# Four graph layers in one kernel: when a chunk of rows is finished, and how far ahead weight tiles are made

## The chip, the cores and the metric

The kernel runs on one core of a Trainium2 chip. The core's engines work side by side, each through its own queue of instructions: TensorE multiplies matrices (PE in the profile, PEld for its weight loads), VectorE (DVE), ScalarE (ACT) and GpSimd (POOL) do elementwise work, and SyncE (SP) issues DMAs; ACT and POOL issue some too. An engine that needs another's result waits for a semaphore. On-chip tiles lie in SBUF, and matmuls write to PSUM. The metric is the device time of one execution in microseconds.

## The reference

`x` has 2708 rows of 512 features, and `adj` is a symmetric 0/1 matrix of 2708 x 2708 with ones on its diagonal. Four layers follow one another, each of the form x = x + layer(relu(layernorm(x)), adj):

```python
# layer 0
support = a.T @ X;  out = relu((support @ weight) * deg**-0.5)
# layer 1: of each row the first 64 neighbours only
keep = Ab & (jnp.cumsum(Ab.astype(jnp.int32), axis=1) <= neibor_num)
nb_mean = (keep @ X) / jnp.maximum(cnt, 1.0)
out = leaky_relu(X @ W_line.T + b_line) + leaky_relu(nb_mean @ W_nb.T + b_nb)
# layer 2: attention with 8 heads of 64
attention = softmax(where(adj > 0, leaky_relu(f1[:, None] + f2[None, :]), -9e15))
out = elu(attention @ Wh)
# layer 3: mean over the neighbours, two linear maps, their concatenation through a third
agg = mask @ x / jnp.maximum(deg, 1.0)
out = relu(concatenate([x @ W_self + b_self, agg @ W_nb + b_nb]) @ W_comb + b_comb)
```

Layers 1 and 3 each multiply a masked adjacency matrix by a 2708 x 512 matrix. The change concerns these two multiplications.

## The kernel before

Rows are worked on in 22 chunks of 128; the last has 20 rows. Layer 0 also packs the adjacency pattern, and the pattern later lies on the chip as bytes (`vT`). Each of layers 1 and 3 has two stages. A dense stage goes through the chunks: it loads x, normalizes it, transposes it on TensorE and multiplies it by the weights. What is to be aggregated is split into two parts of fp32r (`halves`, L291), so that each product of the aggregation is two matmuls. In layer 1 this stage runs from the end of layer 0 to about 508 us.

The second stage is `aggregate` (L432). The chunks that are computed are grouped in seven spans of 4, 4, 4, 4, 3, 2 and 1 chunks (`cuts`, L108). For each span it makes 22 steps, one for each chunk `m` that is summed over. A step needs a weight tile `kt`, which holds the masked pattern between chunk `m` and the chunks of the span: 512, 384, 256 or 128 columns wide. In layer 1, `weight1` (L868) makes it on DVE by comparing `lastr` (the position up to which a row's neighbours are kept) with the index of the row, times the pattern. In layer 3, `weight3` (L1526) makes it by a cast of the pattern. Both pools hold three `kt` buffers. `multiply` then issues two matmuls for each chunk of the span (one where `m` is the short chunk) into that chunk's PSUM accumulator; these are line L424. Thus a step of a four-chunk span is eight matmuls, and one of the one-chunk span is two.

The lines of the program are written out in steps by `staged` (L250): at each step first `make` for the step that lies `lead` ahead, and then `multiply` for the own step. `lead` is 2 in both layers. `multiply` also does three other things. At step 11 it loads the rows of x that the span's result is added to (`before`). In the last span it starts the first three steps of layer 2's dense stage, at steps 9, 13 and 18 (`AHEAD`, L476). And in the first steps of a span it finishes the chunks of the span before, one in each step (`after`).

In layer 1 finishing a chunk (`after1`, L880) is: on DVE, scale the accumulator and add the bias (L883), then the leaky relu (L886), both into `y`; on POOL, add `y` to x (L890); and on the ACT queue, a DMA that saves x. The last span's own chunk is added on DVE. In layer 3 (`after3`, L1568) it is two DVE instructions (L1571, L1574) and the DMA to the output.

A planner orders the instructions of each engine's queue. It goes by the order in which the lines are written and by when it thinks that operands and buffers are there, so a `kt` can stand between L883 and L886 of a chunk, and work of layer 2 between the last steps of layer 1. Tiles of x lie in a ring of five buffers (`XBUFS`, L111), accumulators in a ring of eight PSUM banks. The tiles of layer 2, among them `parts` and `parts2` (L964 and L968, cleared by POOL), take over SBUF that layer 1's tiles held, and wait for the last use of those.

Of the kernel before, what the change touches and what calls it, by code (L numbers as in the profile page):

```python
# [9 lines left out]
F32R = mybir.dt.float32r  # L10
# [12 lines left out]
R = 128  # L23
# [21 lines left out]
def fast_layers(  # L45
# [63 lines left out]
    spans = [list(range(a, b)) for a, b in zip(cuts, cuts[1:])]  # L109
# [3 lines left out]
    WG = KMAX * R  # L113
# [136 lines left out]
    def staged(count, *stages, done=0):  # L250

        for step in range(done, count + max(lag for lag, _ in stages)):
            emit_step(step, count, stages)
# [157 lines left out]
    def pattern(m, cs, n=R):  # L411

        g, k = where[m]
        v = vT[g][:n, k, cs[0] * R : (cs[-1] + 1) * R]
        return v.rearrange("p (c r) -> p c r", r=R)

    def by_chunk(t, cs):
        return t[:, : len(cs) * R].rearrange("p (c r) -> p c r", r=R)

    def matmuls(acc, parts, weight, k, m):  # L420

        q = 2 if m < NC - 1 else 1
        for i in range(q):
            nc.tensor.matmul(  # L424
                acc[:R],
                weight[:, k * R : (k + 1) * R],
                parts[:, i, :],
                start=(m == 0 and i == 0),
                stop=(m == NC - 1),
            )  # L430

    def aggregate(weight_of, parts, before, after, lead=2, ahead=()):  # L432

        units = [(g, m) for g in range(len(spans)) for m in range(NC)]
        weight, loaded, acc = {}, {}, {}

        def make(i):  # L440
            g, m = units[i]
            weight[i] = weight_of(m, spans[g])

        def multiply(i):
            g, m = units[i]
            cs = spans[g]
            if m == 0:
                for c in cs:
                    acc[c] = ps.tile([P, D], F32, name="acc", tag="ps")
            for k, c in enumerate(cs):  # L450
                matmuls(acc[c], parts[m], weight[i], k, m)
            del weight[i]
            if m == NC // 2:
                loaded.update((c, before(c)) for c in cs)
            if g == len(spans) - 1:
                for at_m, fn, *args in ahead:
                    if m == at_m:
                        fn(*args)
            if g and m < len(spans[g - 1]):
                c = spans[g - 1][m]  # L460
                after(c, acc.pop(c), loaded.pop(c))

        staged(len(units), (0, make), (lead, multiply))
        for c in spans[-1]:
            after(c, acc.pop(c), loaded.pop(c))
# [7 lines left out]
    with ExitStack() as ring_ctx:  # L473
# [31 lines left out]
        with tc.tile_pool(name="l0", bufs=2) as wk, ExitStack() as ctx_l0:  # L505
            units = [(g, m) for g in range(len(groups)) for m in range(NC)]
            tiles, acc, sums, xs = {}, {}, {}, {}
# [254 lines left out]
        wk = ring_ctx.enter_context(tc.tile_pool(name="l1", bufs=1, side="right"))  # L762
# [3 lines left out]
        h1, turned = {}, {}  # L766
# [99 lines left out]
            nc.sync.dma_start(w2s[:, f], w2[:, f * P : (f + 1) * P, :].rearrange("h p o -> p h o"))  # L866

        def weight1(m, cs):  # L868
            kt = wk.tile([R, WG], F32R, name="kt", bufs=3)
            nc.vector.scalar_tensor_tensor(  # L870
                by_chunk(kt, cs),
                lastr[:, cs[0] * R : (cs[-1] + 1) * R].rearrange("p (c r) -> p c r", r=R),
                index[:R, m : m + 1],
                pattern(m, cs),
                op0=ALU.is_ge,
                op1=ALU.mult,
            )
            return kt
# [32 lines left out]
            scalar=True,  # L911
        )
        ahead = [(m, emit_step, step, NC, stages2) for step, m in enumerate(AHEAD)]
        aggregate(weight1, h1, before1, after1, ahead=ahead)

# [55 lines left out]
    row, weight, wh, whs, acc, sides, made, scaled = {}, {}, {}, {}, {}, {}, [], {}  # L973
# [499 lines left out]
    with ExitStack() as stack:  # L1473
# [34 lines left out]
        for c in range(NC):  # L1508
# [13 lines left out]
        wk = stack.enter_context(  # L1522
            tc.tile_pool(name="l3", bufs=2, side="right", reuse_waits="tile")
        )
# [645 lines left out]
def kernel(tc: tile.TileContext, *args: bass.AP):  # L2170

    nc = tc.nc
    with tc.tile_pool(name="verdict", bufs=1) as pool:
        verdict = pool.tile([1, 1], I32, name="verdict")
        fast_layers(tc, *args, verdict)
        odd = nc.values_load(verdict[0:1, 0:1], min_val=0, max_val=P + 1)
        with tc.If(odd > 0):
            general_layers(tc, *args)
# [32 lines left out]
```

## Time and profile before

| what | us |
|---|---|
| median of 3 runs (lowest, highest) | 1751.03 (1750.17, 1754.02) |
| the profiled execution | 1754.19 |
| its span, from the first instruction to the last | 1752.3 |
| PE busy | 1724.1 |
| DVE busy | 1312.2 |
| ACT busy | 845.6 |
| POOL busy | 248.3 |
| layer 1's aggregation, in the span's time | 507.9 to 728.9 |
| layer 3's aggregation | 1529.1 to 1745.2 |

In the page, a group of instructions has one row: line, engine and operation, output tile and input tiles, shapes, count, busy time and mean, and at its end the idle time of the engine just before these instructions and what ended it. The chain of work that ended last is followed back from the last instruction. The table by stretch cuts the span where one asks and gives each engine's busy time there, with the number of instructions in brackets. The timeline gives start, length, engine and line of each instruction or run of equal ones, and in square brackets the idle time before it.

### The profile page before, as it was taken

The numbers are of one execution on the slowest core, as the hardware profiler recorded it, in microseconds if no ns is written. First come the engines' busy times: TensorE is split into PE (matmuls) and PEld (weight loads), VectorE is DVE, ScalarE is ACT, GpSimd is POOL, SyncE is SP. The second block draws the span as 40 slices with busy tenths as digits, with TensorE's granted clock in tenths as the row PEclk, the third lists the DMA queues.
The fourth block names the chain that finished last, engine by engine and source line by source line (L and its number), as shares of the span: only waits on it lengthen the run. The fifth ranks groups of instructions, "written<-read, shape, count | busy, mean of one in ns | idle before, by whom it ended". The sixth has DMA issues, their size and how long they took to land.

```text
span 1752.3 us, 29486 instructions
## 1 busy us (share of the span) xinstructions
PE 1724.1 (98%) x11280; PEld 1078.8 (62%) x11280; DVE 1312.2 (75%) x1902; ACT 845.6 (48%) x1554; POOL 248.3 (14%) x252
## 2 busy tenths in 40 slices
PE   8999999999999999999999999999999999999998
PEld 5567777744468887644675665434434455588886
DVE  7759889855455556888899999999998677633334
ACT  5447777622210000366878888888794566400000
POOL 1003323311111112255000000000001222100000
PEclk9999999999999999999999999999999999999999
DMA  8436666444551111332420221022022444313221
GB/s 291 139 117 199 205 206 186 133 120 123 121 135 49 48 49 56 122 122 93 133 63 13 61 64 58 15 64 62 13 74 72 130 141 130 109 36 109 73 72 41
DMA packets 167227, 177.37 MB, mean 101 GB/s; under 512 B 84127, under 2 KB 106591, under 8 KB 166060
## 3 DMA queue, kind: packets, MB, share of 16 engines
q1 hardware_dynamic: 144428, 131.99, 27.2%
q10 hardware_dynamic: 18808, 33.37, 5.1%
q0 software_dynamic: 3840, 10.03, 1.5%
q8 instruction: 90, 1.47, 0.4%
q14 instruction: 61, 0.50, 0.1%
HBM read 111.64 MB, written 55.36 MB: 95 GB/s over the span
## 4 chain that ended last, share of the span: by engine, by line
PE 86%; DVE 8%; ACT 2%; issue 2%; DMA 1%; SPq 1%; POOL 0%; ACTq 0%; DVEq 0%; POOLq 0%
PE acc L424 36%; PE av L1297 17%; PE nb_ps L187 8%; DVE t L1067 5%; PE sums L1297 4%; PE h_ps L187 4%; PE line_ps L187 4%; PE self_ps L187 4%; PE hT_ps L245 2%; PE fused_ps L370 2%; PE wh_ps L187 1%; DVE wh_a L1114 1%; PE av_ps L1250 1%; ACT b L1085 1%; DVE f L1131 1%
## 5 line engine op out<-in xcount | busy, mean ns | idle before, releaser
L1067 DVE SCALAR_TENSOR_TENSOR t<-rb,ec,vT 128x2708 f32<-128x2708 f32 (+2 forms) x214 | 510.4, 2450 | 8.3 <-PE sums L1297 6.2
L1297 PE MATMUL av<-t,whs 128*32 128x451 f32 (+5 forms) x4432 | 445.5, 514 | 6.2 <-DVE t L1067 3.9
L424 PE MATMUL acc<-halves,kt 128*128 128x512 f32 x1848 | 426.5, 391 | 2.4 <-DVE kt L870 2.1
L424 PEld LDWEIGHTS acc<-halves,kt 128*128 128x128 f32 x1848 | 345.2, 188 | 79.7 <-DVE kt L870 6.6
L1085 ACT ACTIVATE b<-t,eb 128x2708 bf16<-128x2708 f32 (+1 forms) x119 | 285.0, 2395 | 33.3 <-DVE t L1067 33.2
L1297 PEld LDWEIGHTS av<-t,whs 128*32 128x32 f32 (+1 forms) x4432 | 193.2, 110 | 167.9 <-issue 118.5
L424 PE MATMUL acc<-halves,ar 128*128 128x512 f32 x924 | 243.6, 414 | 0.0
L424 PEld LDWEIGHTS acc<-halves,ar 128*128 128x128 f32 x924 | 172.6, 188 | 58.2 <-issue 20.6
L223 ACT ACTIVATE ln_rs<-ln_mv,eps 128x1 f32<-128x1 f32 x88 | 25.7, 295 | 306.3 <-DVE ln_mv L221 298.4
L870 DVE SCALAR_TENSOR_TENSOR kt<-lastr,index,vT 128x512 fp32r<-128x512 int16 (+3 forms) x154 | 112.5, 742 | 75.8 <-PE acc L424 75.4
L1528 DVE CAST kt<-vT 128x512 fp32r<-128x512 uint8 (+3 forms) x154 | 56.5, 368 | 131.3 <-PE acc L424 131.2
L1264 POOL TENSOR_SCALAR z<-y 128x512 f32<-128x512 f32 x22 | 44.1, 2005 | 639.5 <-DMA aT<-avT 513.6
L555 DVE TENSOR_TENSOR_SCAN cum<-ai,deg 128x512 int16<-128x512 int32 (+2 forms) x110 | 128.3, 1170 | 0.0
L598 ACT ACTIVATE cum<-cum,limit 128x512 int16<-128x512 int16 (+3 forms) x132 | 88.0, 667 | 51.6 <-DVE deg L563 49.4
L1297 PE MATMUL sums<-t,whs 128*32 128x325 f32 (+4 forms) x952 | 104.4, 451 | 0.0
L1051 ACT ACTIVATE whs<-wh,ef 128x64 f32<-128x64 f32 x214 | 72.5, 342 | 59.6 <-PE sums L1297 21.1
L219 DVE BATCH_NORM_STATS2 ln_st<-x 128x6 f32<-128x512 f32 x88 | 60.3, 687 | 48.3 <-DMA x<-x 34.1
L187 PE MATMUL nb_ps<-wfn,hT 128*128 128x512 f32 x168 | 78.7, 612 | 2.1 <-ACT hT L247 2.1
L187 PE MATMUL wh_ps<-w2s,hT 128*128 128x512 f32 x168 | 76.1, 595 | 1.0 <-ACT hT L247 0.9
L187 PE MATMUL h_ps<-w0s,hT 128*128 128x512 f32 x168 | 76.5, 598 | 0.0
L1297 PE MATMUL sums<-b,parts 128*32 128x338 bf16 (+2 forms) x884 | 76.0, 308 | 0.0
L549 ACT ACTIVATE ar<-ai 128x512 fp32r<-128x512 int32 (+2 forms) x132 | 75.0, 568 | 1.7 <-DMA ai<-in_adj 1.3
(211 smaller groups left out, 1952.7 us busy)
## 6 DMA issues: line engine op xcount, KB each, us to landing
x<-x SPq DMA_DIRECT2D x105, 256.0 KB
ai<-in_adj SPq DMA_DIRECT2D x84, 256.0 KB
x<-x ACTq DMA_DIRECT2D x84, 256.0 KB
x<-in_x SPq DMA_DIRECT2D x42, 256.0 KB
rb<-rT SPq DMA_DIRECT2D x7, 1354.0 KB
wh<-whd SPq DMA_DIRECT2D x63, 96.0 KB
packed<-two POOLq DMA_DIRECT2D x44, 128.0 KB, 3.3
whd<-wh SPq DMA_DIRECT2D x21, 256.0 KB
```

What stands on the lines that cost most here:

```text
L187: nc.tensor.matmul(po[:n], lhsT[:, f, :n], w[:, f, :], start=(f == 0), stop=(f == NF - 1))
L219: nc.vector.bn_stats(st[:n], xc[:n])
L424: nc.tensor.matmul(acc[:R], weight[:, k * R : (k + 1) * R], parts[:, i, :], start=(m == 0 and i == 0), stop=(m == NC - 1),)
L549: nc.scalar.activation(ar[:, :gw], ai[:, :gw], AF.Square, accum_out=squares[:R, m, g : g + 1])
L555: nc.vector.tensor_tensor_scan(cum[:n, :gw], ai[:n, :gw], ai[:n, :gw], 0.0 if g == 0 else deg[:n, m : m + 1], op0=ALU.add, op1=ALU.max,)
L598: nc.scalar.activation(cum[:n, :gw], cum[:n, :gw], AF.Sign, bias=limit[:n], scale=-1.0, accum_out=signs[:n, m, g : g + 1],)
L870: nc.vector.scalar_tensor_tensor(by_chunk(kt, cs), lastr[:, cs[0] * R : (cs[-1] + 1) * R].rearrange("p (c r) -> p c r", r=R), index[:R, m ...
L1051: ins = nc.scalar.activation(t[:q, :O], wh.pop((u, m))[:q], AF.Copy, scale=by)
L1067: ins = nc.vector.scalar_tensor_tensor(t[:q, : hi - lo], row[h][:q, lo:hi], ec[:q, m, h : h + 1], vT[g][:q, k, lo:hi], op0=ALU.max, op1=AL ...
L1085: nc.scalar.activation(b[:q, : hi - lo], weight[s][:, : hi - lo], AF.Sigmoid, bias=eb[:q, m, h : h + 1], scale=STEEP,)
L1297: nc.tensor.matmul(p[j * S : (j + 1) * S, : b - a], lhsT, rhs[:, part * size + a : part * size + b], start=(s % NC == 0), stop=(s % NC == ...
L1528: nc.vector.tensor_copy(by_chunk(kt, cs), pattern(m, cs))
```

## The change

Two edits are made. In `aggregate` a chunk of the span before is finished in each step while the new span has three or four chunks, as it was; in each second step where the span has two chunks (steps 0, 2 and 4 of layer 1's and layer 3's sixth span); and in each third step where it has one (steps 0 and 3 of the seventh). In layer 1 alone, weight tiles are made four steps ahead and their pool has five buffers. Layer 3 keeps two steps and three buffers.

```diff
@@ aggregate
-            if g and m < len(spans[g - 1]):
-                c = spans[g - 1][m]
-                after(c, acc.pop(c), loaded.pop(c))
+            if g:
+                k, off = divmod(m, 1 + 2 // len(cs))
+                if off == 0 and k < len(spans[g - 1]):
+                    c = spans[g - 1][k]
+                    after(c, acc.pop(c), loaded.pop(c))
@@ weight1
-            kt = wk.tile([R, WG], F32R, name="kt", bufs=3)
+            kt = wk.tile([R, WG], F32R, name="kt", bufs=5)
@@ the call in layer 1
-        aggregate(weight1, h1, before1, after1, ahead=ahead)
+        aggregate(weight1, h1, before1, after1, lead=4, ahead=ahead)
```

## The prediction

> **What bounds the kernel now.** I read the page's busy shares first, then its chain, then the table by stretch for the spans concerned, then the timeline inside them. From the page:
>
> ```profile
> span 1752.3 us, 29486 instructions
> PE 1724.1 (98%) x11280; PEld 1078.8 (62%) x11280; DVE 1312.2 (75%) x1902; ACT 845.6 (48%) x1554; POOL 248.3 (14%) x252
> L424 PE MATMUL acc<-halves,kt 128*128 128x512 f32 x1848 | 426.5, 391 | 2.4 <-DVE kt L870 2.1
> L424 PEld LDWEIGHTS acc<-halves,kt 128*128 128x128 f32 x1848 | 345.2, 188 | 79.7 <-DVE kt L870 6.6
> ```
>
> TensorE sets the time nearly everywhere. A matmul's end is modelled, so the 2.1 us on the first L424 row understates the waits on `kt`; the 6.6 us on the row of weight loads overstates them, since part of each is hidden under matmuls still in flight. The table by stretch, for instructions that touch `kt` (length, PE busy, weight loads, DVE busy), settles it; the rows are layer 1's wide spans, its two-chunk and one-chunk spans, then layer 3's two-chunk and one-chunk spans:
>
> ```profile
> 507.90:693.30 185.40, 185.40 (x817) 152.90 (x817) 88.50 (x109) 1.00 0.19 58
> 693.30:714.80 21.50, 20.17 (x87) 15.79 (x86) 11.93 (x23) 1.00 0.24 76
> 714.80:728.90 14.10, 12.36 (x45) 7.46 (x43) 7.96 (x21) 1.00 0.34 94
> 1714.50:1734.00 19.50, 19.50 (x87) 16.14 (x86) 6.13 (x23) 1.00 0.18 59
> 1734.00:1744.90 10.90, 10.82 (x45) 7.76 (x43) 4.58 (x21) 1.00 0.12 48
> ```
>
> The wide spans give the pace: 185.40 us / 817 = 0.227 us a matmul. At that pace a two-chunk span (86 weight loads) is 19.5 us and a one-chunk span (43) is 9.8 us. So layer 1 loses 21.5 - 19.5 = 2.0 us in its two-chunk span. Its one-chunk span holds other TensorE work too: 8 transposes at 0.11 us (the chain has four in 0.44 us) and 2 matmuls of layer 2 at 0.43 us (eight in 3.45 us), 1.7 us together; it loses 14.1 - 9.8 - 1.7 = 2.6 us. Layer 3 loses nothing in the two-chunk span and 10.9 - 9.8 = 1.1 us in the last. All that this change can win directly is 5.7 us of 1752.3.
>
> Why they are lost, from the timeline (start, length, engine, line):
>
> ```profile
> 697.50 0.74 DVE L883 SCALAR_TENSOR_TENSOR y<-acc,rcnt,bn 128x512 f32<-128x512 f32 x1
> 697.71 1.27 POOL L890 TENSOR_TENSOR x<-x,y 128x512 f32<-128x512 f32 x1 [1.02 <-DVE y L886]
> 698.16 1.10 DVE L870 SCALAR_TENSOR_TENSOR kt<-lastr,index,vT 128x256 fp32r<-128x256 int16 x1
> 699.18 0.68 DVE L886 SCALAR_TENSOR_TENSOR y<-y 128x512 f32<-128x512 f32 x1
> 699.32 0.76 PEld L424 LDWEIGHTS acc<-halves,kt 128*128 128x128 f32 x4 [1.52 <-DVE kt L870]
> 699.79 2.69 DVE L870 SCALAR_TENSOR_TENSOR kt<-lastr,index,vT 128x256 fp32r<-128x256 int16 x4
> 700.00 1.41 POOL L890 TENSOR_TENSOR x<-x,y 128x512 f32<-128x512 f32 x1 [1.02 <-DVE y L886]
> ...
> 718.78 2.16 DVE L870 SCALAR_TENSOR_TENSOR kt<-lastr,index,vT 128x128 fp32r<-128x128 int16 x4
> 718.99 1.27 POOL L890 TENSOR_TENSOR x<-x,y 128x512 f32<-128x512 f32 x1 [0.88 <-DVE y L886]
> 720.46 1.70 PEld L424 LDWEIGHTS acc<-halves,kt 128*128 128x128 f32 x8 [0.99 <-DVE kt L870]
> ```
>
> Finishing chunks (L883, L886) stand between the `kt` tiles in DVE's queue, and a `kt` that starts while the POOL add L890 runs lasts until that add ends: 1.10 us at 698.16 where an undisturbed one takes 0.48. L883 at 697.50 runs its normal 0.74 us across the same add.
>
> **The skill.** The Trainium skill, "SBUF — State Buffer", section "Who interferes with whom": a DVE instruction with two SBUF inputs contends with a GpSimd instruction that reads SBUF, and the later one is blocked until the first ends. The trace agrees: `kt` reads two SBUF tiles and is held, by up to 1.03 us; L883 reads PSUM and one tile and isn't. "Perfetto Trace Analysis", section "Optimization Strategy", says that repeated bubbles on the engine that should be full can mean too few buffers; here they come in short runs after each change of span, so buffers and the finishing work both bear on them.
>
> **The change, part by part.** No instruction is added or removed and no DMA either; the order and one buffer count change.
>
> *Four ahead, five buffers (layer 1).* In the two-chunk span a buffer is free 1.31 us after its step began (four loads of 0.227 us, and 0.39 us for the last matmul), the new tile needs 0.45 us, and a step lasts 0.907 us. With three buffers the tile is wanted 3 x 0.907 = 2.72 us after that beginning, which leaves 0.96 us of cover; with five, 4.53 - 1.76 = 2.77 us. In the one-chunk span (step 0.454 us, free after 0.85 us, tile 0.35 us) cover goes from 0.16 to 1.07 us.
>
> *The DVE debt against it.* From 693.41 to 701.98 (8.57 us) DVE makes seven `kt` at 0.39 us from start to start (2.73), finishes three chunks at 0.66 + 0.60 us (3.78) and is held for 2.1 us: 5.9 us of debt. Free DVE time is 0.907 - 0.39 = 0.52 us a step, so about 3.1 us is paid in the six steps that pass, and 5.9 - 3.1 = 2.8 us meets the cover. Before: 2.8 - 0.96 = 1.9 us of waiting, against 2.0 seen. After: 2.8 against 2.77, and spread over steps 0, 2 and 4 the debt comes later, so it never stands there at once. I count the whole 2.0 us as won.
>
> *The one-chunk span.* Two chunks cost 2 x 1.26 us, and `kt` is held 0.36 + 1.02 us: 3.9 us, with only 0.454 - 0.26 = 0.19 us a step to pay it. Cover grows by 0.91 us. Finishing in steps 0 and 3 pays another 2 x 0.19 = 0.4 us, but it also takes away an overlap: now L883 of the second chunk runs under the first chunk's add (716.88 under 716.83), and only 0.36 us of holding is left; three steps later a `kt` will stand there and may be held 1.02 us, 0.7 us more. The gain lies between 0.91 + 0.4 - 0.7 = 0.6 and 1.3 us; I take 0.8, near the low end, since several `kt` now stand ready behind each L886.
>
> *Layer 3.* It keeps two ahead and only spreads. Its finishing is 0.67 + 0.61 us a chunk, all on DVE, no POOL add. Now four tiles in a row come late (0.23, 0.29, 0.34, 0.28 us between 735.15 and 737.42). With the second chunk two steps later the first two delays, 0.5 us, stay, and about 0.3 comes back later: 0.8 of 1.1, so 0.3 us is won (bounds 0 and 0.6).
>
> *Moved at no cost, and their cover.* The saves (ACT queue) follow their adds; chunk 20's goes later in steps and earlier or equal in time. Its x tile holds up layer 2's fourth load, whose statistics ran at 722.99 and whose product TensorE reaches some 12 us later (three chunks of 3.87 us): that is the cover. The two added buffers take 4 KB a partition more, so other tiles of the layer-1 pool move; the two POOL memsets at the end (1.30 and 0.78 us; the second already waited 8.67 us for the last L883) may both follow the last L883. The first POOL product comes 2 us after that, so at most about 1 us shows; I take 0. In the wide spans cover was already enough (185.40 us without a gap), so there is nothing to win there.
>
> Sum: 2.0 + 0.8 + 0.3 = 3.1 us of the profiled 1752.3 us span: 1749.2. That execution took 1754.19 us with what lies around the span; the median of the runs is 1751.03, so the forecast is 1747.9 us. It passes through layer 2 because TensorE is 100% busy from 729 to 768.
>
> **Rivals.**
> *All of it.* The holding overlaps other work and both spans run at pace: 2.0 + 2.6 + 1.1 = 5.7 us, 1745.3. For it: the cover of 1.07 us is as long as one holding. Against it: 3.9 us of debt in a span that pays 0.19 us a step.
> *Swallowed at layer 2's entry.* TensorE uses some of today's waits for transposes and products of layer 2, and the chain from 735 to 768 goes by DVE (L1114, L1131, L219) and loads of x, not TensorE; the first gap of TensorE there, 0.49 us, is at 768.4. If that loop moves by only 0.8 us, 0.8 us is all that is won, 1750.2. For it: DVE is 13.2 of 14.0 us busy in the one-chunk span. Against it: the loop begins with a product of TensorE, which moves.
> *Slower.* Today four chunks' statistics for layer 2 (L219 at 721.51, 722.99, 724.61, 727.01, about 1.0 us each with what follows) are squeezed between late `kt` tiles. If tiles made four ahead push them past the end of layer 1, DVE owes 4.0 us when the loop starts, and each chunk's x buffer is freed later, one load (3.51 us in the chain) with it: 7.5 - 3.1 = 4.4 us slower, 1755.4. It decides once more than about three of the four slip.
>
> **How the numbers follow.** Changes under 0.2% (3.5 us) can hardly be told from none. Forecast 0.37, with 1.5 us either way, so 0.45 of it lies beyond 3.5 us; all of it 0.30; swallowed 0.17; slower 0.16, of which 0.02 stays within 3.5 us. Faster: 0.30 + 0.17 = 0.47. Slower: 0.14. Same: 0.39. The likeliest case alone is 1746.4 to 1749.4. For eight in ten I go from just under "all of it" to short of the slower case: 1744.6 to 1754.2.
>
> **What would show it.** Right: the two-chunk span of layer 1 takes 19.5 to 20 us, its one-chunk span about 13.3, layer 3's last about 10.6; and `kt` rows right behind an L886 still last over 1 us. "All of it" shows 9.8 us plus 1.7 in the one-chunk span. Swallowed: layer 1 ends 3 us sooner, but gaps of TensorE appear before 768. Slower: rows of L219 after the last `kt`, and weight loads of `wh_ps` waiting for `hT`. I'd be wrong if the order of DVE's queue differs from the one argued here, or if layer 2's later work falls into another order.

## The result

The changed kernel takes 1747.88 us (median of 22 runs, 1745.59 to 1750.86); the kernel before took 1751.99 us (median of 22 runs, 1748.98 to 1754.19). The ratio is 0.9978, with a 95% interval of 0.9972 to 0.9984. By the ratio it is 3.9 us faster, between 2.8 and 4.9; the two medians are 4.1 us apart. The profiled executions are 8.1 us apart in span. That is more than the change: the one of before lies 2.2 us above its median and the one of after (1746.11 us) 1.8 us below its own. So I compare stretches of the traces, not their ends.

The page of the changed kernel, in the rows that answer to those shown of before. In this kernel the lines after `aggregate` have moved by two: L870 is now L872, L883 is L885, L886 is L888, L890 is L892.

```profile
span 1744.2 us, 29465 instructions
PE 1718.2 (99%) x11280; PEld 1077.2 (62%) x11280; DVE 1310.1 (75%) x1902; ACT 845.2 (48%) x1554; POOL 248.8 (14%) x252
L424 PE MATMUL acc<-halves,kt 128*128 128x512 f32 x1848 | 423.6, 390 | 1.0 <-DVE kt L872 1.0
L424 PEld LDWEIGHTS acc<-halves,kt 128*128 128x128 f32 x1848 | 346.0, 188 | 75.4 <-DVE kt L872 2.6
```

The weight loads' wait for layer 1's tiles fell from 6.6 to 2.6 us. The table by stretch, again for instructions that touch `kt` (layer 1's wide spans, its two-chunk and one-chunk spans, layer 3's two-chunk and one-chunk spans):

```profile
507.60:692.50 184.90, 184.90 (x816) 153.06 (x816) 87.81 (x109) 1.00 0.19 58
692.50:712.00 19.50, 19.50 (x87) 16.10 (x86) 11.56 (x23) 1.00 0.19 70
712.00:724.30 12.30, 11.12 (x44) 7.69 (x43) 7.75 (x19) 1.00 0.35 114
1707.20:1726.70 19.50, 19.50 (x87) 16.14 (x86) 6.14 (x23) 1.00 0.18 59
1726.70:1736.90 10.20, 10.19 (x44) 7.84 (x43) 4.48 (x21) 1.00 0.13 51
```

The two-chunk span runs at the matmuls' pace: 19.5 us, where it took 21.5. The one-chunk span took 12.3 us. It now holds four transposes (0.4 us) and no product of layer 2, so it still loses 12.3 - 9.8 - 0.4 = 2.1 us, where it lost 2.6. Layer 3's last span loses 0.4 us, where it lost 1.0: counted from its first weight load to the end of its last, that span took 10.8 us before, and the stretch of 10.9 us in the prediction's table ends 0.1 us late.

What is left in the one-chunk span, from the timeline:

```profile
713.81 1.91 DVE L872 SCALAR_TENSOR_TENSOR kt<-lastr,index,vT 128x128 fp32r<-128x128 int16 x3
714.03 1.28 POOL L892 TENSOR_TENSOR x<-x,y 128x512 f32<-128x512 f32 x1 [12.18 <-DVE y L888]
715.51 0.77 PEld L424 LDWEIGHTS acc<-halves,kt 128*128 128x128 f32 x4 [0.82 <-DVE kt L872]
...
717.17 3.74 DVE L872 SCALAR_TENSOR_TENSOR kt<-lastr,index,vT 128x128 fp32r<-128x128 int16 x9
717.38 1.28 POOL L892 TENSOR_TENSOR x<-x,y 128x512 f32<-128x512 f32 x1 [2.07 <-DMA x<-x]
718.85 3.96 PEld L424 LDWEIGHTS acc<-halves,kt 128*128 128x128 f32 x18 [1.00 <-DVE kt L872]
```

Three tiles from 713.81 on take 1.91 us together. Undisturbed, a tile starts 0.26 us after the one before it, and the last one takes 0.34 us, which makes 0.86 us for three. So they are held for about 1.0 us while the POOL add runs, and TensorE's loads then wait 0.82 us for a tile. The second add, at 717.38, does the same, and the loads wait 1.00 us.

### The profile page after: what moved, and what is told of

It is laid out like the page before. It is cut to its first block, busy times and chain, and to the rows that moved or that the text cites. A ratio compares the mean times of both kernels' runs of the same rounds, so it can differ in the third digit from the quotient of the medians.

```text
span 1744.2 us, 29465 instructions
## 1 busy us (share of the span) xinstructions
PE 1718.2 (99%) x11280; PEld 1077.2 (62%) x11280; DVE 1310.1 (75%) x1902; ACT 845.2 (48%) x1554; POOL 248.8 (14%) x252
## 4 chain that ended last, share of the span: by engine, by line
PE 42%; DVE 8%; issue 3%; ACT 2%; DMA 2%; SPq 1%; POOL 0%; ACTq 0%; DVEq 0%; POOLq 0%
PE av L1299 16%; PE acc L424 12%; DVE t L1069 6%; PE nb_ps L187 4%; PE self_ps L187 4%; PE sums L1299 4%; DMA x<-x 1%; PE wh_ps L187 1%; DVE wh_a L1116 1%; PE hT_ps L245 1%; ACT b L1087 1%; DVE f L1133 1%; PE av_ps L1252 1%; DVE ln_st L219 0%; DMA rb<-rT 0%
## 5 line engine op out<-in xcount | busy, mean ns | idle before, releaser
L872 DVE SCALAR_TENSOR_TENSOR kt<-lastr,index,vT 128x512 fp32r<-128x512 int16 (+3 forms) x154 | 112.6, 746 | 72.3 <-PE acc L424 72.0
L219 DVE BATCH_NORM_STATS2 ln_st<-x 128x6 f32<-128x512 f32 x88 | 60.3, 687 | 49.5 <-DMA x<-x 35.2
```

What stands on the lines that cost most here:

```text
L219: nc.vector.bn_stats(st[:n], xc[:n])
L872: nc.vector.scalar_tensor_tensor(by_chunk(kt, cs), lastr[:, cs[0] * R : (cs[-1] + 1) * R].rearrange("p (c r) -> p c r", r=R), index[:R, m ...
```

## The experiments

The first theory says that layer 1's waits come from DVE's debt against the cover that the buffers give, so that the longer lead removes them, and that what stays in the one-chunk span is the hold by POOL's add. A rival says that the spreading removes them. A second rival says that the larger pool alone does, by free buffers or by moved addresses.

### One part alone

```diff
 # lead_only: the kernel before, with
-            kt = wk.tile([R, WG], F32R, name="kt", bufs=3)
+            kt = wk.tile([R, WG], F32R, name="kt", bufs=5)
-        aggregate(weight1, h1, before1, after1, ahead=ahead)
+        aggregate(weight1, h1, before1, after1, lead=4, ahead=ahead)
```

> Only the weight tiles of layer 1 four steps ahead with five buffers; chunks are finished in each step, as before. If cover is what removes the waits: layer 1's two-chunk span 19.5 to 19.7 us (21.5 before), its one-chunk span loses 1.5 to 2.2 us beyond its matmuls, layer 3's last span stays at 10.9 us; ratio to before about 0.9982. If spreading is what removes them: the two-chunk span stays above 20.5 us and the ratio is 0.9995 or more.

```diff
 # spread_only: the kernel before, with
-            if g and m < len(spans[g - 1]):
-                c = spans[g - 1][m]
-                after(c, acc.pop(c), loaded.pop(c))
+            if g:
+                k, off = divmod(m, 1 + 2 // len(cs))
+                if off == 0 and k < len(spans[g - 1]):
+                    c = spans[g - 1][k]
+                    after(c, acc.pop(c), loaded.pop(c))
```

> Only the spreading, in both layers; weight tiles two steps ahead with three buffers. If cover is what removes the waits: layer 1's two-chunk span still about 20.6 us, its one-chunk span no better than before (2.6 us lost, or up to 0.7 more, since the second chunk's L883 no longer runs under the first one's POOL add), layer 3's last span 10.2 us as in the changed kernel; ratio about 0.9993. If spreading removes them: 19.5 us in the two-chunk span and a ratio of 0.998.

```diff
 # bufs_only: the kernel before, with
-            kt = wk.tile([R, WG], F32R, name="kt", bufs=3)
+            kt = wk.tile([R, WG], F32R, name="kt", bufs=5)
```

> Only the five buffers; tiles are still written out two steps ahead. If free buffers are enough because the planner makes any tile whose buffer is free: the same as with the lead, 19.5 us in the two-chunk span. If the order in which the lines are written decides: tiles still stand behind the finishing work, and the spans take 21.5 us and 14.1 us as before, ratio 1.000. A ratio away from both would show what the moved SBUF addresses do.

Measured: `lead_only` 1747.72 us, ratio 0.9982 (0.9975 to 0.9989); `spread_only` 1750.83 us, 0.9998 (0.9990 to 1.0006); `bufs_only` 1751.37 us, 0.9996 (0.9987 to 1.0004). The tables by stretch for `kt`, of `lead_only` (layer 1's two-chunk and one-chunk spans, layer 3's last):

```profile
692.40:712.15 19.75, 19.75 (x88) 16.07 (x87) 11.51 (x23) 1.00 0.26 83
712.15:723.85 11.70, 10.60 (x45) 7.83 (x43) 7.05 (x19) 1.00 0.34 113
1726.70:1737.50 10.80, 10.73 (x45) 7.75 (x43) 4.56 (x21) 1.00 0.13 49
```

and of `spread_only`:

```profile
692.98:714.02 21.04, 20.55 (x88) 15.60 (x86) 12.32 (x23) 1.00 0.18 65
714.02:727.44 13.42, 11.98 (x44) 7.38 (x43) 8.54 (x21) 1.00 0.37 118
1730.80:1741.00 10.20, 10.19 (x45) 7.84 (x43) 4.47 (x21) 1.00 0.13 51
```

The lead does nearly all of layer 1. With it alone the two-chunk span is 19.75 us, and the one-chunk span, with four transposes, loses 11.7 - 9.8 - 0.4 = 1.5 us. With the spreading alone the two-chunk span is still 21.0 us (I had expected 20.6), and the one-chunk span, with six transposes, loses 13.42 - 9.76 - 0.66 = 3.0 us. So in the one-chunk span the spreading costs 0.4 us without the lead (3.0 against 2.6) and 0.6 us with it (2.1 against 1.5). In the two-chunk span it gives 0.5 us without the lead and 0.2 us beside it. What it does win is layer 3's last span, 10.8 to 10.2 us. Beside the lead these gains and this cost nearly cancel: the whole change (ratio 0.9978) can't be told from the lead alone (0.9982).

The timeline of `lead_only` shows what the spreading takes away in the one-chunk span:

```profile
714.15 1.29 POOL L890 TENSOR_TENSOR x<-x,y 128x512 f32<-128x512 f32 x1 [13.59 <-DVE y L886]
714.20 0.74 DVE L883 SCALAR_TENSOR_TENSOR y<-acc,rcnt,bn 128x512 f32<-128x512 f32 x1
714.86 0.73 DVE L870 SCALAR_TENSOR_TENSOR kt<-lastr,index,vT 128x128 fp32r<-128x128 int16 x1
```

The second chunk's L883 runs under the first chunk's add, so the tile behind it is held for 0.4 us only (0.73 us against 0.34). In the changed kernel tiles stand there, and they are held for 1.0 us.

Buffers without the earlier order win little. In `bufs_only` the planner puts the finishing work of two chunks in one piece ahead of the next tile, as the timeline of DVE, and the load that waits for it, show:

```profile
693.43 1.40 DVE L883 SCALAR_TENSOR_TENSOR y<-acc,rcnt,bn 128x512 f32<-128x512 f32 x2
694.75 1.28 DVE L886 SCALAR_TENSOR_TENSOR y<-y 128x512 f32<-128x512 f32 x2
695.95 1.50 DVE L870 SCALAR_TENSOR_TENSOR kt<-lastr,index,vT 128x256 fp32r<-128x256 int16 x1
697.50 0.77 PEld L424 LDWEIGHTS acc<-halves,kt 128*128 128x128 f32 x4 [0.64 <-DVE kt L870]
```

Its two-chunk span takes 21.15 us, 0.4 us less than before. Its wide spans take 185.2 us where they took 185.6; every trace of a kernel with five buffers has this gain, and `spread_only` does not. Together that is 0.9 us, too little for its total to show. The length of its one-chunk span isn't read, since TensorE's clock was halved for 3.4 us in it.

### A second trace of both kernels

The edit in each is an empty line at the end of the file.

> The kernel before with an empty line added at its end: ratio 1.000. Its trace is a second look at the same program: if the 5 us by which the attention stage and layer 3's dense stage differ between the two profiled executions of before and after are chance, these stages come out near those of the changed kernel here, or in between; if they are the change's doing, they come out as in the first profile of before.

> The changed kernel with an empty line added: the ratio of the changed kernel, 0.9978. Its trace is a second look: layer 1's spans 19.5 and 12.3 us and layer 3's last 10.2 us, as in the first; what differs by more than 0.2 us between the two looks in layer 2 or in layer 3's dense stage is chance.

Measured: 1751.42 us, ratio 1.0000 (0.9992 to 1.0009), and 1747.91 us, ratio 0.9982 (0.9975 to 0.9988). Layer 1's and layer 3's spans repeat within 0.04 us in both. Layer 2's third chunk, the first that lies wholly behind the handover, begins its product at 735.87 and 735.61 us before, and at 732.64 and 733.10 after: 2.9 us earlier. The last chunk's product ends layer 2's dense stage 2.8 us earlier (812.75 against 809.95, the means of two traces each). So what layer 1 wins is kept through that stage. Later stages vary between two executions of one program. From there to the start of layer 3's dense stage it took 541.3 and 539.9 us before, and 539.1 and 540.6 after, so the difference of the first profiles in layer 2's attention is chance. Layer 3's dense stage took 174.2 and 175.4 us before, and 172.9 and 172.8 after. This second difference repeats in these four traces, but the other traces show that it goes with TensorE's clock; the last section comes back to it.

### The hold by POOL's add

```diff
 # after_dve_add: the changed kernel, with
-            eng = nc.vector if c in spans[-1] else nc.gpsimd
+            eng = nc.vector if c >= spans[-3][0] else nc.gpsimd
```

> The changed kernel with the adds of chunks 16 to 20 (L892) on DVE, not on POOL. If the held tiles are what is left in layer 1's one-chunk span: no kt lasts over 0.5 us there, DVE owes 2 x 1.86 = 3.7 us instead of 2.5 + 2.1 = 4.6, and the loss falls from 2.1 to about 1.2 us, so the ratio is about 0.0005 under that of the changed kernel. If they are not: DVE has 1.2 us more to do and the loss rises to about 3.3 us.

```diff
 # after_no_add: the changed kernel, with
-            eng.tensor_tensor(xc[:n], xc[:n], y[:n], ALU.add)
+            if c not in spans[-2]:
+                eng.tensor_tensor(xc[:n], xc[:n], y[:n], ALU.add)
```

> The changed kernel without the adds of layer 1's result to x for chunks 19 and 20 (the two that are finished in the one-chunk span), so these rows of x2 lack it. If the hold by POOL's add is the cause of what is lost there: DVE owes only 2 x 1.26 = 2.5 us, and with 1.07 us of cover and 0.19 us a step the loss is 0.5 us or less (2.1 with the adds). If DVE's own finishing work is the cause, it stays above 1.5 us.

```diff
 # before_dve_add: the kernel before, with
-            eng = nc.vector if c in spans[-1] else nc.gpsimd
+            eng = nc.vector if c >= spans[-3][0] else nc.gpsimd
```

> The kernel before with only the adds of chunks 16 to 20 moved to DVE. By the sums of DVE time: the held time before was 2.1 us over three adds and 1.4 over two, and an add on DVE costs 0.6 us, so the two-chunk span is 0.3 us shorter (21.2) and the one-chunk span 0.2 (its loss 2.4 us): ratio 0.9997. If the hold by POOL were the chief cause of the waits before, the ratio would be below 0.9988.

Measured: `after_dve_add` 1745.06 us, ratio 0.9967 (0.9954 to 0.9979); `after_no_add`, one execution, 1745.49 us; `before_dve_add` 1752.80 us, ratio 1.0008 (1.0000 to 1.0017). In `after_dve_add` the adds run on DVE and the tiles behind them at their normal length (timeline, then the table for `kt` in the two-chunk and one-chunk spans):

```profile
714.04 0.68 DVE L892 TENSOR_TENSOR x<-x,y 128x512 f32<-128x512 f32 x1
714.64 0.60 DVE L872 SCALAR_TENSOR_TENSOR kt<-lastr,index,vT 128x128 fp32r<-128x128 int16 x2
```

```profile
692.52:712.01 19.49, 19.49 (x88) 16.14 (x86) 9.69 (x23) 1.00 0.20 70
712.01:723.10 11.09, 10.80 (x45) 7.76 (x43) 5.82 (x19) 1.00 0.38 120
```

With seven transposes in it (0.8 us), the one-chunk span loses 0.5 to 0.6 us; I had expected about 1.2. DVE was given more instructions to do in this span and TensorE waits 1.5 us less there: most of what was left was the hold, not DVE's own work. The total fell further, 2.8 us below that of `after_again`, but this comparison flatters it. All six of its executions were granted a mean TensorE clock of 0.997 or 0.998 of full speed. Of the 20 of `after_again`, the eleven with such a clock have a median of 1747.1 us, which leaves 2.0 us. Without the two adds the span takes 10.45 us with four transposes and loses 0.2 to 0.3:

```profile
713.15:723.60 10.45, 10.34 (x44) 7.92 (x43) 5.69 (x19) 1.00 0.08 26
```

Its two-chunk span, ahead of the adds that were left out, took 20.2 us, 0.7 more than with them. The timeline shows one wait:

```profile
708.03 0.69 DVE L219 BATCH_NORM_STATS2 ln_st<-x 128x6 f32<-128x512 f32 x1 [1.25 <-DMA x<-x]
709.17 3.50 PEld L424 LDWEIGHTS acc<-halves,kt 128*128 128x128 f32 x16 [0.88 <-DVE kt L872]
```

A statistic of layer 2 stands ahead of a tile in DVE's queue and waits for its rows of x until 708.03. In the changed kernel they were there at 706.87, and no load waited. So only the one-chunk span is read from this run.

On the kernel before the same move wins nothing, as its ratio shows. Its two-chunk and one-chunk spans:

```profile
693.16:714.98 21.82, 20.17 (x88) 15.91 (x86) 10.07 (x23) 1.00 0.21 75
714.98:730.26 15.28, 12.73 (x44) 7.52 (x43) 6.82 (x21) 1.00 0.28 88
```

I had expected both to be a little shorter. They are 0.3 and 1.2 us longer; four products of layer 2 stand in the second instead of two, which is 0.9 us of the 1.2. Without tiles made ahead, an add on DVE delays the next tile just as a held tile does. Nor does the sum of DVE's time give the sign: over the two spans DVE is busy for 30.5 us in both kernels, and the order decided.

### Layer 3's lead, and all together

```diff
 # after_l3_lead: the changed kernel, with
-            kt = wk.tile([R, WG], F32R, name="kt3", bufs=3)
+            kt = wk.tile([R, WG], F32R, name="kt3", bufs=4)
-        aggregate(weight3, h3, before3, after3)
+        aggregate(weight3, h3, before3, after3, lead=3)
```

> The changed kernel with layer 3's weight tiles three steps ahead and four buffers. Its last span still loses 0.4 us in the changed kernel: three loads wait for a cast, the first right after the first L1573. With one more step of cover (0.454 us) the loss is 0 to 0.1 us and the span 9.8 to 9.9 us, 0.3 us less; nothing else moves, so the ratio is that of the changed kernel within 0.0005. If the casts wait for something else than a buffer, the span stays at 10.2 us.

`after_both` joins this with the edit of `after_dve_add`. `mixed` is `after_both` without the spreading in layer 1:

> The changed kernel with both additions: adds of chunks 16 to 20 on DVE, and layer 3's tiles three steps ahead with four buffers. The two act at different places, so their gains add: layer 1's spans 19.5 and 11.1 us, layer 3's last 9.8 us; ratio to before 0.9965, the fastest so far. If one takes back what the other gives, a span comes out longer than it did alone.

> As both additions, but layer 1 finishes a chunk in each step again. If spreading helps once no tile is held by POOL: the two chunks' 3.7 us of DVE work come together in the one-chunk span against 1.07 us of cover, so its loss is about 1.2 us (0.6 with spreading), and the two-chunk span takes up to 0.3 us more. If spreading in layer 1 is of no use at all, both spans are as with it.

Measured: `after_l3_lead` 1747.06 us, ratio 0.9977 (0.9969 to 0.9985); `after_both` 1745.57 us, 0.9963 (0.9950 to 0.9977); `mixed` 1745.83 us, 0.9966 (0.9952 to 0.9979). Layer 3's last span in `after_l3_lead`:

```profile
1727.30:1737.05 9.75, 9.75 (x45) 8.00 (x43) 4.07 (x20) 1.00 0.14 54
```

Layer 3's last span runs at the matmuls' pace. In `after_both` the three spans are 19.49, 11.07 and 9.79 us, so the two gains add. In `mixed` layer 1's spans are 19.98 and 11.50 us, 0.5 and 0.4 us more, of which one more transpose is 0.1 (I had expected up to 0.3, and 0.6). So once no tile is held, spreading in layer 1 does pay. That agrees with its cost in the changed kernel coming from the hold. The totals of these two can't be told apart. `after_both` has the lowest ratio of all, 6.5 us under the kernel before (4.0 to 8.8); it can't be told from `after_dve_add`, which has the lowest median.

## Why the prediction was right, and where it was off

The forecast was 1747.9 us and the median is 1747.88. That they agree so closely is luck. The forecast started from 1751.03 us, the median of three executions, where 22 of them give 1751.99; and it took off 3.1 us, where the medians are 4.1 apart. The two errors of 1.0 us cancelled. The terms, read from the traces, are sound in the main:

*The two-chunk span.* All 2.0 us were to go, by a cover of 2.77 us against 2.8 us of debt. It takes 19.5 us: right. `lead_only` (19.75 us) and `spread_only` (21.0 us) show that the cover does it, with 0.2 us from the spreading. (The working's 2.8 - 0.96 is 1.8 us, not 1.9; nothing hangs on it.)

*The one-chunk span.* I took 0.8 us from a range of 0.6 to 1.3. The loss fell by 0.5 us, from 2.6 to 2.1, just below that range. The mechanism was right, both ways: cover won 1.1 us (`lead_only`: 1.5 lost), where I had 0.91, and the spreading gave 0.6 us back, where I had 0.3 net. The extra hold of 0.7 us came about; the 0.4 us of slack that was to be paid against it brought at most 0.1. Where nothing is held (`mixed` against `after_both`) spreading is worth 0.3 us in this span. The length of about 13.3 us given as a sign was off by 1.0 us, because I kept eight transposes and two products in the span, and the planner left four transposes and no product.

*Layer 3.* I took 0.3 us, with bounds of 0 and 0.6; it won 0.6 us, the upper bound. The two delays after the first chunk stayed, as said. The timeline of the changed kernel shows that next to nothing came back at the second:

```profile
1727.85 0.30 PEld L424 LDWEIGHTS acc<-halves,kt 128*128 128x128 f32 x2 [0.27 <-DVE kt L1530]
1728.59 1.68 PEld L424 LDWEIGHTS acc<-halves,kt 128*128 128x128 f32 x8 [0.44 <-DVE kt L1530]
1730.43 6.22 PEld L424 LDWEIGHTS acc<-halves,kt 128*128 128x128 f32 x28 [0.16 <-DVE kt L1530]
```

*The wide spans.* "There is nothing to win there" was wrong. They took 185.6 us before and 185.1 us after. I had taken the pace from that very stretch and so hidden a wait in it. The three-chunk span of before shows it:

```profile
668.06 3.71 POOL L890 TENSOR_TENSOR x<-x,y 128x512 f32<-128x512 f32 x2 [0.89 <-DVE y L886]
668.97 1.65 DVE L870 SCALAR_TENSOR_TENSOR kt<-lastr,index,vT 128x384 fp32r<-128x384 int16 x1
670.67 0.99 PEld L424 LDWEIGHTS acc<-halves,kt 128*128 128x128 f32 x5 [0.36 <-DVE kt L870]
```

A held tile of 384 columns came late there too. The 0.5 us went with the two added buffers: it is gone in `bufs_only` as in `lead_only`, and stays in `spread_only`.

The sum by stretches is 0.5 + 2.0 + 0.5 + 0.6 = 3.6 us, where I had 3.1, and the runs say 3.9 (2.8 to 4.9). The second set of runs, `after_again`, says 3.2 (0.0018 of 1751.31; 2.1 to 4.4).

*The moves at no cost.* The POOL memsets did go behind the last finishing work: L967 at 727.50 and L971 at 728.74, with a third of 0.39 us before them. They end at 729.8, and the first product of POOL starts at 730.66, 0.9 us later; nothing was delayed by them. "It passes through layer 2" held: 2.9 us at its third chunk, 2.8 us at its last.

*The rivals.* "All of it" asked that the holding overlap other work, and TensorE still waits for held tiles. That most of what it missed in layer 1 was due to the add is shown by `after_dve_add`, whose one-chunk span loses 0.6 us. "Swallowed" fell at layer 2's last chunk; nor did the gaps appear that it foretold before 768 us: TensorE is busy without a break from 724.3 to 757.0 us, and from there to 768.5 it stands still for 0.2 us, where before it was 0.6. "Slower" would have needed rows of L219 standing after the last tile. The last tile starts at 722.88; two of the four, at 720.82 and 722.30, stand before it, and two, at 723.28 and 725.61, slipped behind it. In the kernel before, all four stood before the last tile. Two is fewer than the three that would have decided, and layer 2 was not later for them.

## What to carry to other kernels

Where a bounded ring of tiles feeds the bounding engine, work out its cover: the time from a buffer's release to when its next tile is needed, less the time to make that tile. Set against it what stands ahead of the tile in the producer's queue; three buffers that nearly suffice in a wide span leave 0.16 us in a narrow one. More buffers are worth little if the tiles are still written out behind the work that delays them (`bufs_only`). Spreading that work is not free either: if part of it holds the producer through another engine, it can take away an overlap that hid the hold, so move the holding instruction first and then spread. And take a matmul's pace from consecutive weight loads, not from a long stretch that may hide waits.

## What the runs showed that I had not expected

TensorE ran at half its clock for pieces of 3.4 us, sometimes two or three in a row, and their number and place differ between executions of the same program. The granted clock in the 30 us from shortly before layer 3's dense stage was 0.83 in the first profile of before:

```profile
1345.00:1375.00 30.00, 24.88 (x112) 11.93 (x109) 21.28 (x47) 16.16 (x24) 6.54 (x5) 0.83 0.40 116
```

and 0.94 in the same stage of the first profile of after:

```profile
1339.00:1369.00 30.00, 24.89 (x143) 12.18 (x136) 23.50 (x53) 16.82 (x26) 7.85 (x5) 0.94 0.44 131
```

That is (1 - 0.83) x 30 / 0.5 = 10.2 us at half clock against some 3.5; the second traces of both were granted 0.89 over 30 us there. The Trainium skill, "TensorE: Matmul & The Clock Gate", section "Part 1: The HAM clock gate (the "warmup" mystery)", describes a gate that halves TensorE's clock after an idle window of about 3.4 us. The length of the pieces agrees. But the stretch ahead of a piece wasn't wholly idle here: ahead of the one in layer 1's one-chunk span of `bufs_only`, TensorE was busy for 1.50 of 3.45 us by the profile (PE is the first number after the length, the granted clock the third from the end):

```profile
716.30:719.75 3.45, 1.50 (x8) 0.74 (x6) 3.45 (x4) 0.82 (x1) 2.87 (x2) 1.00 0.15 35
719.75:723.16 3.41, 3.24 (x8) 2.57 (x9) 2.65 (x9) 0.60 (x1) 0.00 (x0) 0.50 0.67 225
```

The length of layer 3's dense stage goes with these pieces. In the four traces where half clock falls at the start of the stage and ends within 3.5 us of it (`after`, `after_again`, `after_l3_lead`, `lead_only`), the stage takes 172.8 to 172.9 us. In the six where a single piece comes about 11 us into it, it takes 173.7 to 174.0. Three of these six have none or only a part of the change (`before_dve_add`, `bufs_only`, `spread_only`); the others (`after_dve_add`, `after_both`, `mixed`) have the longer lead, two of them the whole change. `after_no_add`, with a piece at both places, takes 174.3. The two traces of before, 174.2 and 175.4, have 10.2 us and 6.8 us at half clock around there. So what repeated in four traces is no gain of the change. Whether the change moves the pieces can't be told from thirteen traces.

Nor do the pieces make the result. Over whole executions the granted clock and the time go together: in the 22 of the changed kernel, the seven at 0.995 or 0.996 have a median of 1750.1 us and the fifteen at 0.997 or 0.998 one of 1746.9. Among executions at 0.997 or 0.998 measured together, the kernel before took 1750.9 us (27) and `after_again` 1747.1 (11): 3.8 us, close to the 3.6 of the stretches.
